# Seven block products for a graph product, spread over a batch of an attention loop

## The chip, the cores and the metric

The kernel runs on one core of a Trainium2 chip. A core has five engines with a queue each: TensorE (PE, matrix products; its weight loads are listed as PEld), VectorE (DVE), ScalarE (ACT), GpSimd (POOL) and SyncE (SP, which here only issues DMAs). Each engine works through its own queue in order, and semaphores make one queue wait for another. The metric is the time of one execution on the device, in microseconds, from the first to the last instruction and what lies around them; lower is better.

## The reference

Two layers work on 16 batches of 1024 rows by 256 channels, all in fp32. The change lies in the first layer and touches its seams to the second. Cut to what matters:

```python
def layer0(x, para, adj, kv_w):            # x: (16, 1024, 256)
    fea = transpose(x, (0, 2, 1))
    c = mean(fea, axis=1)                  # mean over channels, one per row
    diff = c[:, None, :] - c[:, :, None]
    A = abs(abs(sigmoid(diff) - 0.5) - 0.5) * 2.0
    A_s = (A + transpose(A, (0, 2, 1))) * 0.5
    g = einsum('bcn,bnm->bcm', fea, adj[None] * A_s)   # the graph product
    g = relu(g * para.reshape(1, 256, 1024))
    q = g transposed, 4 heads of 64
    k, v = x @ kv_w, 4 heads of 64
    attn = softmax(q k^T * scale)
    return attn @ v

x = layernorm(x + layer0(x, ...))
x = layernorm(x + layer1(x, ...))          # adjacency average, two linear layers, batchnorms
```

## The kernel before

A batch is 1024 rows in eight chunks of 128 partitions (`NCH`), so a batch's x is a tile of 128 x 8 x 256. Everything of the first layer runs in one loop over *bursts*. A *unit* is one head pair (64-channel heads, two at a time), one half of the queries and one chunk of 128 keys; a batch has 32 units, a burst is two of them, and so a batch has 16 bursts, called 0 to 15 here (`u` in the code). Bursts 0 to 7 are head pair 0, bursts 8 to 15 head pair 1.

In each burst PE first computes the scores of the burst's two units (`scores`, L903), for which ACT takes the exponential (L908); then the outputs of the burst before (`outputs`, L924), beside which DVE sums the exponentials into `acc` (L931, L933), one accumulation of 1024 wide a unit and none for the first unit of a query half. When a query half is through (once in four bursts), ACT copies half of its output (L937) and DVE adds the other half (L938). When a head pair is through, `normalise` multiplies `acc` with ones on PE (L946) to get the denominators, ACT copies them out (L952), and SP sends them through DRAM to be turned into columns. Some bursts later `residual` transposes the outputs back on PE (L970), DVE scales them (L974), and POOL adds them to x (L979). After the second head pair's residual, `finish_x1` does the layernorm on DVE (L596, L597, L600, with a power on POOL, L589) and POOL stores the result.

Beside this attention of batch b, the loop prepares batch b+1. That preparation is a list of steps made by `prologue`:

- `begin` (L747 to L756): DVE sums x over channels, SP sends the means through DRAM and spreads them as a row `crow` over all partitions.
- `transpose_x` (L765, L768): PE transposes x into `xT`, DVE copies it out of PSUM.
- `keys` (L842, copied by ACT L846) and `values` (L855, copied by DVE L859).
- the weights of the graph product, in place in eight tiles `wg` of 128 x 1024: `weights_abs` on ACT (L784), `weights_tanh` on ACT (L789), `weights_adj` on DVE (L793, times the adjacency).
- `graph_mm` (L805): four results (two channel halves by two query halves), each of eight matmuls over the chunks, 32 in all; then `queries`: DVE multiplies by para and the scale (L814), ACT takes the relu (L817). Batch 0 has `graph_first` instead, which runs before the loop.

Which step is run in which burst is written out by hand. The sets `FULL` and `SIDE` say it: in bursts 0, 4, 6, 8, 10 and 12 four steps each of keys, values and graph matmuls, with transposes of the next batch but one in bursts 10 and 12; in bursts 13, 14, 15, 1, 2, 3 and beside the steps of 0 and 4 the abs, tanh and adjacency products. The queues of PE, ACT and DVE keep that written order within a stage; POOL and SP wait for data and buffers alone.

Buffers set the rest of the order. PSUM has two tiles of 1024 for scores (`tile_s`), two banks for everything else that is copied out (`tile_t`: transposes, keys, values, graph results, denominators, residuals), which alternate, and two for outputs. There are four tiles for exponentials (`pp`), one buffer `xT`, one `crow`, eight `wg`, three of x.

After the loop, the second layer builds its averaged features, from batch 1 on with a scheme of seven block products in place of eight (`left_sums` on POOL, L659 to L662; `right_sums` on DVE, L666 to L669; `products`).

Of the kernel before, what the change touches and what calls it, by code (L numbers as in the profile page):

```python
# [515 lines left out]
def fast_path(  # L516
# [74 lines left out]
    def layernorm(t, name):  # L591
        st = small.tile([P, NCH, 6], F32, tag="ln_st", name=f"st_{name}")
        mv = small.tile([P, NCH, 2], F32, tag="ln_mv", name=f"mv_{name}")
        rstd = small.tile([P, NCH], F32, tag="ln_rs", name=f"rs_{name}")
        for n in range(NCH):
            nc.vector.bn_stats(st[:, n, :], t[:, n, :])  # L596
            nc.vector.bn_aggr(mv[:, n, :], st[:, n, :])  # L597
        rsqrt(rstd, mv[:, :, 1], EPS)
        for n in range(NCH):
            nc.vector.tensor_scalar(  # L600
                t[:, n, :], t[:, n, :], mv[:, n, 0:1], rstd[:, n : n + 1], ALU.subtract, ALU.mult
            )

# [96 lines left out]
    with (  # L700
        tc.tile_pool(name="l0c", bufs=1) as l0c,
        tc.tile_pool(name="qkv", bufs=2) as qkv,
# [30 lines left out]
        def prologue(b):  # L733


            s = st[b]
            xt = s["x"]
            first, steps, side = [], [], []

            def step(f, *a):  # L740
                steps.append((f, a))
# [16 lines left out]
            def transpose_x(c, half):  # L758
                if c == 0 and half == 0 and b:
                    begin()  # L760
                if c == 0 and half == 0:
                    s["xT"] = xTp.tile([P, CC, N], F32, tag="xT", name=f"xT_{b}")
                pt = tile_t(f"pxT_{b}_{c}_{half}")
                for j in range(4):
                    nc.tensor.transpose(  # L765
                        pt[:, j * P : (j + 1) * P], xt[:, 4 * half + j, c * P : (c + 1) * P], ident
                    )
                nc.vector.tensor_copy(s["xT"][:, c, half * HALF : (half + 1) * HALF], pt)  # L768
# [28 lines left out]
            def graph_mm(c, half, part):  # L797
                if part == 0:
                    s["pg"] = tile_t(f"pg_{b}_{c}_{half}")
                    if c == 0 and half == 0:  # L800
                        s["qT"] = qkv.tile([P, CC, N], F32, tag="qT", name=f"qT_{b}")
                ps = s["pg"]
                hs = slice(half * HALF, (half + 1) * HALF)
                for n in (2 * part, 2 * part + 1):
                    nc.tensor.matmul(  # L805
                        ps, xt[:, n, c * P : (c + 1) * P], s["wg", n][:, hs],
                        start=(n == 0), stop=(n == NCH - 1),
                    )
                if part == 3:
                    queries(c, hs, ps)  # L810

            def queries(c, hs, ps):
                q = s["qT"][:, c, hs]
                nc.vector.scalar_tensor_tensor(  # L814
                    q, ps, -scale, para_s[:, c, hs], op0=ALU.mult, op1=ALU.mult
                )
                nc.scalar.activation(q, q, AF.Relu)  # L817

            def graph_first(n):

                if n == 0:
                    both = tile_s("pg_0_0")
                    s["pg"] = [both[:, H0], both[:, H1], tile_o("pg_0_1_0"), tile_o("pg_0_1_1")]
                    s["qT"] = qkv.tile([P, CC, N], F32, tag="qT", name="qT_0")
# [6 lines left out]
                if n == NCH - 1:  # L831
                    for c in range(CC):
                        for half, hs in enumerate((H0, H1)):
                            queries(c, hs, s["pg"][2 * c + half])

            def keys(kc, half):
                if kc == 0 and half == 0:
                    s["kT"] = qkv.tile([P, CC, N], F32, tag="kT", name=f"kT_{b}")
# [7 lines left out]
                nc.scalar.copy(s["kT"][:, kc, hs], ps)  # L846

            def values(pair):
                if pair == 0:
                    s["v"] = qkv.tile([P, NCH, C], F32, tag="v", name=f"v_{b}")  # L850
                pt = tile_t(f"pv_{b}_{pair}")
                for j in range(2):
# [6 lines left out]
                nc.vector.tensor_copy(  # L859
                    s["v"][:, 2 * pair : 2 * pair + 2, :].rearrange("p n c -> p (n c)"), pt  # L860
                )

            for i in range(2 * CC):
                first.append((transpose_x, (i // 2, i % 2) if b else (i % 2, i // 2)))
            if b == 0:
                first += [(begin, ()), (row_of_means, ())]
            for i in range(4):
                step(values, i)
                step(keys, i // 2, i % 2)
            for c in range(CC):  # L870
                for half in range(2):
                    for part in range(4):
                        if b:
                            step(graph_mm, c, half, part)
            for n in range(NCH if b == 0 else 0):
                step(graph_first, n)
            for n in range(NCH):
                side.append((weights_abs, (n,)))
                side.append((weights_tanh, (n,)))
                if n:  # L880
                    side.append((weights_adj, (n - 1,)))
            side.append((weights_adj, (NCH - 1,)))
            return first, steps, side
# [11 lines left out]
        def scores(i):  # L895
            b, pr, qh, m = units[i]
            qT, kT = st[b]["qT"], st[b]["kT"]
            ps = tile_s(f"ps_{i}")
            for kh in range(2):
                for hd in range(2):  # L900
# [3 lines left out]
                        ps[kh * D : (kh + 1) * D, hd * HALF : (hd + 1) * HALF], kT[r, pr, ks],  # L904
                        qT[r, pr, qh * HALF : (qh + 1) * HALF], start=True, stop=True,
# [34 lines left out]
        def normalise(b, pr):  # L940
# [10 lines left out]
            row = rdp.tile([P, HALF], F32, tag="drow", name=f"drow_{k}")  # L951
# [28 lines left out]

        def finish_x1(b):
            xt = st.pop(b)["x"]
            layernorm(xt, f"l0_{b}")
            nc.gpsimd.dma_start(x1_d[b], xt)
# [129 lines left out]
        FULL = (0, 4, 6, 8, 10, 12)  # L1114
        SIDE = {13: 2, 14: 2, 15: 2, 1: 2, 2: 2, 3: 2}
        with tc.manual_schedule(engines={mybir.EngineType.PE, mybir.EngineType.Activation, mybir.EngineType.DVE}):


            first, steps, side = prologue(0)
            run(first, 6)  # L1120
            next_first, next_steps, next_side = prologue(1)
            for _ in range(8):
                run(steps, 1)
                run(side, 2)
            run(next_first, 4)
            for n in range(NCH):
                run(side, 2)
                run(steps, 1)
                if n:
                    run(next_side, 3)  # L1130
            run(next_side, 99)
            run(next_steps, 8)
            full, sums, late = {}, {}, {}

            def back(j):
# [4 lines left out]
                if m == NCH - 1 and qh == 1:  # L1140
                    sums.setdefault(j + 1, []).append((normalise, (b, pr)))
                    for q in range(2):
                        full.setdefault(j + 5, []).append((residual, (b, pr, q)))
                    if pr == PAIRS - 1:
                        late.setdefault(j + 6, []).append((finish_x1, (b,)))
# [5 lines left out]
                8: [(transpose_adjacency, (m, h)) for m in (6, 7) for h in (0, 1)],  # L1151
                5: [(load_x1l, (0,))],
# [7 lines left out]
                6: [(adjacency_rows, (n,)) for n in (0, 1, 2)] + [(load_weights, ())],  # L1160
# [4 lines left out]
            for j in range(len(bursts)):  # L1165
# [3 lines left out]
                if u == 0:  # L1169
                    steps, side = next_steps, next_side  # L1170
                    next_first, next_steps, next_side = [], [], []
# [3 lines left out]
                if u == 5 and b + 2 < B:  # L1175
                    load_x(b + 2)
                    next_first, next_steps, next_side = prologue(b + 2)
                if u in FULL:
                    if u >= 10:
# [406 lines left out]
```

## Time and profile before

| what | value |
|---|---|
| median of three runs | 2655.48 us (2652.28 to 2655.86) |
| the profiled execution | 2653.06 us |
| its span, first to last instruction | 2651.3 us |
| before the attention loop | 75.4 us |
| attention loop, batches 1 to 13 | 104.9 us each |
| from the last burst to the end | about 1020 us |

A line of a profile names the source line, the engine, the operation and its tiles by the program's names, output first. A fp32 matmul of the source shows as two passes in the profile, so 32 matmuls of a batch are 64. Groups give a mean duration of one; where instructions of an engine follow each other without a wait, the next can start before the first has ended. The idle time of an engine that isn't on the path that sets the end costs nothing.

In the page's slices of the span, an engine's busy share is a digit (tenths) for each of 40 stretches of 66 us; the attention loop fills stretches 2 to 26:

```profile
DVE  5465665756656657666566576765655655533376
ACT  5363563654645636545446354410101001233368
POOL 0001000100100011001000100321222211100044
```

In the loop DVE is busy for some six tenths, ACT for five, POOL for less than one.

### The profile page before, as it was taken

How to read it: one execution, taken by the hardware profiler on the slowest of the kernel's cores; microseconds unless marked ns; L12 is line 12 of the kernel's file. 1: busy time of each engine (PE TensorE's matmuls, PEld its weight loads, DVE VectorE, ACT ScalarE, POOL GpSimd, SP SyncE). 2: the span in 40 equal slices, each digit the busy share in tenths (PEclk: the TensorE clock that was granted, in tenths of full speed). 3: DMA queues.
4: the chain of work that ended last, by engine and by line, in shares of the span. 5: the costliest groups of instructions: out<-in, count | busy, mean ns of one | idle time of the engine just before them, and what ended most of it. 6: DMA issues, size and time to landing. Idle time of an engine off the chain costs nothing. (4 is left out here: it accounts for less than half of the span.)

```text
span 2651.3 us, 31994 instructions
## 1 busy us (share of the span) xinstructions
PE 2553.7 (96%) x12966; PEld 1110.1 (42%) x12966; DVE 1600.2 (60%) x2160; ACT 1126.8 (43%) x1349; POOL 336.2 (13%) x407
## 2 busy tenths in 40 slices
PE   8999999999999999999999999999999999999964
PEld 4443444444434434444444343344444444444443
DVE  5465665756656657666566576765655655533376
ACT  5363563654645636545446354410101001233368
POOL 0001000100100011001000100321222211100044
PEclk9999999999999999999999999999999999999975
DMA  4001101001011011010110110112122122353367
GB/s 143 2 9 41 33 10 41 21 22 33 9 41 33 9 41 33 10 41 3 39 33 9 41 49 1 41 64 95 80 95 95 66 92 82 137 202 143 149 222 240
DMA packets 134557, 168.94 MB, mean 64 GB/s; under 512 B 86785, under 2 KB 120065, under 8 KB 124033
## 3 DMA queue, kind: packets, MB, share of 16 engines
q1 hardware_dynamic: 129568, 116.47, 14.2%
q0 software_dynamic: 4832, 50.34, 4.6%
q8 instruction: 103, 1.69, 0.3%
q14 instruction: 54, 0.43, 0.0%
HBM read 99.36 MB, written 67.44 MB: 63 GB/s over the span
## 5 line engine op out<-in xcount | busy, mean ns | idle before, releaser
L908 ACT ACTIVATE p<-ps 128x1024 f32<-128x1024 f32 x512 | 495.7, 1020 | 179.5 <-PE ps L903 142.9
L933 DVE TENSOR_TENSOR acc<-acc,p 128x1024 f32<-128x1024 f32 x384 | 483.2, 1258 | 61.0 <-ACT p L908 32.4
L903 PE MATMUL ps<-qT,kT 64*64 64x512 f32 x4096 | 490.6, 594 | 1.4 <-ACT p L908 1.4
L924 PE MATMUL po<-p,v 64*64 64x512 f32 x4096 | 485.3, 589 | 0.0
L805 PE MATMUL pg<-wg,x 128*128 128x512 f32 x960 | 425.2, 596 | 0.0
L979 POOL TENSOR_TENSOR x<-x,o 128x512 f32<-128x512 f32 x64 | 109.5, 1711 | 1434.8 <-DVE o L974 1434.8
L924 PEld LDWEIGHTS po<-p,v 64*64 64x64 f32 x4096 | 156.7, 133 | 282.8 <-issue 282.6
L805 PEld LDWEIGHTS pg<-wg,x 128*128 128x128 f32 x960 | 177.6, 190 | 226.9 <-issue 203.3
L903 PEld LDWEIGHTS ps<-qT,kT 64*64 64x64 f32 x4096 | 146.1, 132 | 280.2 <-issue 231.5
L817 ACT ACTIVATE qT<-qT 128x512 f32<-128x512 f32 x64 | 40.3, 631 | 482.0 <-DVE qT L814 481.9
L1456 PE MATMUL po<-hl,w12T 128*128 128x512 f32 x512 | 220.3, 592 | 3.1 <-ACT hl L1387 2.3
L814 DVE SCALAR_TENSOR_TENSOR qT<-pg,para_s 128x512 f32<-128x512 f32 x64 | 43.9, 689 | 271.1 <-PE pg L805 269.8
L793 DVE SCALAR_TENSOR_TENSOR wg<-wg,adj_s 128x1024 f32<-128x1024 f32 x128 | 153.1, 1217 | 15.5 <-ACT wg L789 15.5
L784 ACT ACTIVATE wg<-crow,ccol 128x1024 f32<-128x1024 f32 x128 | 146.6, 1146 | 11.8 <-DMA crow<-c 11.8
L1456 PEld LDWEIGHTS po<-hl,w12T 128*128 128x128 f32 x512 | 97.1, 190 | 126.3 <-issue 120.5
L789 ACT ACTIVATE wg<-wg 128x1024 f32<-128x1024 f32 x128 | 135.5, 1060 | 2.6
L1387 ACT ACTIVATE hl<-hl,bn_sh,bn_sg 128x1024 f32<-128x1024 f32 x64 | 74.3, 1229 | 135.0 <-DMA hl<-h 133.6
L855 PE MATMUL pv<-kvw_s,xT 128*128 128x256 f32 x512 | 124.0, 385 | 1.6 <-ACT kT L846 1.6
L1460 DVE TENSOR_SCALAR o<-po,col_b 128x1024 f32<-128x1024 f32 x32 | 41.1, 1284 | 139.1 <-PE po L1456 139.1
L842 PE MATMUL pk<-xT,kvw_s 128*128 128x512 f32 x256 | 120.3, 592 | 0.0
L855 PEld LDWEIGHTS pv<-kvw_s,xT 128*128 128x128 f32 x512 | 94.9, 190 | 51.9 <-issue 27.6
L1286 PE MATMUL a_agg<-ahT,x1l 128*128 128x512 f32 x240 | 108.1, 593 | 1.1 <-ACT agg L1104 1.1
(151 smaller groups left out, 2625.4 us busy)
## 6 DMA issues: line engine op xcount, KB each, us to landing
h<-hw POOLq DMA_DIRECT2D x16, 2048.0 KB, 6.6
hl<-h SPq DMA_DIRECT2D x15, 2048.0 KB
x<-x POOLq DMA_DIRECT2D x16, 1024.0 KB, 4.2
x1l<-x SPq DMA_DIRECT2D x16, 1024.0 KB
xf<-x SPq DMA_DIRECT2D x16, 1024.0 KB
out_dram<-o SPq DMA_DIRECT2D x16, 1024.0 KB
x<-in_x_dram SPq DMA_DIRECT2D x15, 1024.0 KB
crow<-c SPq DMA_DIRECT2D x15, 512.0 KB
```

Source lines behind the costliest of these rows:

```text
L784: nc.scalar.activation(w, s["crow"], AF.Abs, bias=s["ccol"][:, n : n + 1])
L789: nc.scalar.activation(w, w, AF.Tanh, scale=0.5)
L793: nc.vector.scalar_tensor_tensor(w, w, 1.0, adj_s[:, n, :], op0=ALU.subtract, op1=ALU.mult)
L805: nc.tensor.matmul(ps, xt[:, n, c * P : (c + 1) * P], s["wg", n][:, hs], start=(n == 0), stop=(n == NCH - 1),)
L842: nc.tensor.matmul(ps, kvw_s[:, c, kc * P : (kc + 1) * P], s["xT"][:, c, hs], start=(c == 0), stop=(c == CC - 1),)
L855: nc.tensor.matmul(pt[:, j * C : (j + 1) * C], s["xT"][:, c, n * P : (n + 1) * P], kvw_s[:, c, C : 2 * C], start=(c == 0), stop=(c == CC - 1),
L903: nc.tensor.matmul(ps[kh * D : (kh + 1) * D, hd * HALF : (hd + 1) * HALF], kT[r, pr, ks], qT[r, pr, qh * HALF : (qh + 1) * HALF], start=Tr ...
L908: nc.scalar.activation(p, ps, AF.Exp)
L924: nc.tensor.matmul(g["po"][kh][hd * D : (hd + 1) * D, :], s["v"][r, m, h * D : (h + 1) * D], p[r, hd * HALF : (hd + 1) * HALF], start=(m = ...
L933: nc.vector.tensor_add(g["acc"], g["acc"], p)
L979: nc.gpsimd.tensor_tensor(xs, xs, o.rearrange("p n h d -> p n (h d)"), ALU.add)
L1456: nc.tensor.matmul(ps[:, hs], w2T[:, k, c * P : (c + 1) * P], h[k][:, hs], start=(k == 0), stop=(k == HC - 1),)
```

## The change

The change rewrites the preparation of a batch and its places in the loop.

The graph product of batches 1 to 15 is made of seven block products of four matmuls each (`graph`, `product`), 28 matmuls in place of 32. For it DVE forms four sums of the weights (`right_first` to `right_fourth`, 16 subtractions of 512 wide a batch), and POOL four sums of x (`left`, 512 wide), which lie in the buffer of `xT`. The seven results are added up in the query tiles by one ACT copy and seven DVE additions; the product with para moves to POOL (`times_para`, four a batch), and the scale goes into ACT's relu.

The weights of batch b+2 are begun in bursts 11 to 15 of batch b (abs and tanh), their products with the adjacency follow about one burst behind the tanh, the sums behind these, into burst 6 of the next batch. The graph products sit in bursts 4 (one), 6, 8 and 10 (two each), the transposes of x in burst 10, keys and values in bursts 12 and 14, just ahead of the batch's attention. One half of the copies of `xT` and of the values goes from DVE to ACT.

The layernorm is split: statistics (DVE, POOL) five bursts after the last burst of a batch, the last step two bursts later and on ACT, as eight Identity activations with scale and bias. The residual of the second head pair comes one burst earlier. Query and key tiles are held by head pair, three buffers each; the row of denominators shares a buffer with the scaled outputs; loading the second layer's weights moves from batch 14 to batch 15; two small tiles of statistics move into other pools. Before the loop, batch 1's transposes, keys and values are no longer made; batch 0's order is changed a little.

```diff
     def layernorm(t, name):
...
+        def statistics():
+            for n in range(NCH):
+                nc.vector.bn_stats(st[:, n, :], t[:, n, :])
+                nc.vector.bn_aggr(mv[:, n, :], st[:, n, :])
+            rsqrt(rstd, mv[:, :, 1], EPS)
+            nc.gpsimd.tensor_tensor(nmr, mv[:, :, 0], rstd, ALU.mult)
+            nc.gpsimd.tensor_scalar(nmr, nmr, -1.0, None, ALU.mult)
+
+        def apply(n):
+            nc.scalar.activation(
+                t[:, n, :], t[:, n, :], AF.Identity,
+                bias=nmr[:, n : n + 1], scale=rstd[:, n : n + 1],
             )
...
-                nc.vector.tensor_copy(s["xT"][:, c, half * HALF : (half + 1) * HALF], pt)
+                copy = nc.scalar.copy if half and b else nc.vector.tensor_copy
+                copy(s["xT"][:, c, half * HALF : (half + 1) * HALF], pt)
...
+            def right_first(i):
...
+                nc.vector.tensor_sub(S["t1"][:, i, :], w[:, H1], w[:, H0])
+
+            def right_second(i):
+                nc.vector.tensor_sub(S["t2"][:, i, :], s["wg", i + LOW][:, H1], S["t1"][:, i, :])
...
+            def left(k):
+                if k == 0:
+                    S["l"] = xTp.tile([P, 4, LOW, P], F32, tag="xT", name=f"xS_{b}")
...
+                nc.gpsimd.tensor_tensor(l[k], one, two, op)
+
+            def product(k):
+                ps = tile_t(f"pg_{b}_{k}")
+                w = [s["wg", i] for i in range(NCH)]
+                for i in range(LOW):
+                    one, two = {
+                        1: lambda: (xt[:, i, C0], w[i][:, H0]),
...
+                        7: lambda: (S["l"][:, 2, i, :], w[i][:, H1]),
+                    }[k]()
+                    nc.tensor.matmul(ps, one, two, start=(i == 0), stop=(i == LOW - 1))
+                return ps
...
+            def times_para(c, half):
...
+                nc.gpsimd.tensor_tensor(q, q, para_s[:, c, hs], ALU.mult)
...
+                if k == 5:
+                    nc.vector.tensor_add(u, ps, u)
+                    nc.vector.tensor_add(v, ps, v)
+                    times_para(1, 1)
+                if k == 3:
+                    nc.vector.tensor_add(u, ps, u)
+                    times_para(0, 1)
...
+                copy = nc.scalar.copy if pair % 2 and b else nc.vector.tensor_copy
+                copy(s["v"][:, 2 * pair : 2 * pair + 2, :].rearrange("p n c -> p (n c)"), pt)
...
+                "kv": [
+                    (values, (0,)), (keys, (0, 0)), (values, (1,)), (keys, (0, 1)),
+                    (values, (2,)), (values, (3,)), (keys, (1, 0)), (keys, (1, 1)),
+                ],
...
+                "graph": [(graph, (k,)) for k in (1, 6, 2, 7, 4, 5, 3)],
...
+            for i in range(LOW):
+                two = (i, i + LOW)
+                for n in two:
+                    side += [(weights_abs, (n,)), (weights_tanh, (n,))]
+                todo["adj"] += [(weights_adj, (n,)) for n in two]
+                todo["sums"] += [(f, (i,)) for f in (right_first, right_second)]
+            todo["sums"] += [(f, (i,)) for f in (right_third, right_fourth) for i in range(LOW)]
...
+                    wait = 5 if j == len(bursts) - 1 or pr == 0 else 4
                     for q in range(2):
-                        full.setdefault(j + 5, []).append((residual, (b, pr, q)))
+                        full.setdefault(j + wait, []).append((residual, (b, pr, q)))
                     if pr == PAIRS - 1:
-                        late.setdefault(j + 6, []).append((finish_x1, (b,)))
+                        late.setdefault(j + 5, []).append((statistics_x1, (b,)))
+                        late.setdefault(j + 7, []).append((finish_x1, (b,)))
...
+                if u < 4:
+                    part("left", 1)
+                part("side", 99 if u == 0 else 0)
+                part("adj", {0: 1, 1: 99}.get(u, 0))
+                part("sums", {0: 1, 1: 3, 2: 2, 3: 1, 4: 1, 5: 2, 7: 99}.get(u, 0))
+                if u == 4:
+                    part("graph", 1)
+                elif u == 6:
+                    part("graph", 2)
+                    part("sums", 2)
+                elif u == 7:
+                    part("relu", 1)
+                elif u == 8:
+                    part("graph", 2)
+                elif u == 9:
+                    run(after.get("begin", []), 1)
+                elif u == 10:
+                    part("graph", 2)
+                    part("xT", 4)
+                elif u == 11:
+                    part("relu", 3)
+                    run(after["side"], 4)
+                elif u == 12:
+                    for i in range(4):
+                        part("kv", 1)
+                        run(after["side"], 1 + i % 2)
+                        run(after["adj"], i % 2)
+                elif u == 13:
+                    run(after["side"], 2)
+                    run(after["adj"], 2)
+                elif u == 14:
+                    for i in range(4):
+                        part("kv", 1)
+                        run(after["side"], 1)
+                        run(after["adj"] if i % 2 else after["sums"], 1)
+                elif u == 15:
+                    run(after["adj"], 1)
+                    run(after["sums"], 2)
+                run(full.get(j, []), 9)
```

## The prediction

> **What bounds the kernel now.** I read the page's head first, then stages by windows, then the attention loop burst by burst, then the timeline where engines hand over.
>
> ```profile
> PE 2553.7 (96%) x12966; PEld 1110.1 (42%) x12966; DVE 1600.2 (60%) x2160; ACT 1126.8 (43%) x1349; POOL 336.2 (13%) x407
> ...
> 267.30:372.20 104.90, 104.31 (x679) 43.57 (x675) 66.49 (x88) 54.76 (x63) 9.45 (x7) 1.00 0.10 26
> ```
>
> The second line is one batch of the attention loop (length, then busy time of PE, weight loads, DVE, ACT, POOL): PE works 104.3 of 104.9 us, so every wait added to PE is lost time. Batches 1 to 13 all take 104.9; batch 0 takes 87.0, batch 14 104.5, batch 15 74.1 to its last burst's scores. The loop starts at 75.4. Cut at its 16 bursts, one batch reads (bursts 4, 5, 6, 8, 12):
>
> ```profile
> 708.87:720.83 11.96, 11.72 (x69) 6.47 (x61) 7.12 (x10) 6.38 (x8) 0.00 (x0) 1.00 0.00 0
> 720.83:724.31 3.48, 3.48 (x33) 1.28 (x36) 2.21 (x4) 1.94 (x2) 2.64 (x2) 1.00 0.00 0
> 724.31:734.92 10.61, 10.61 (x52) 4.03 (x45) 8.12 (x26) 1.94 (x2) 3.35 (x4) 1.00 0.06 22
> ...
> 738.40:750.01 11.61, 11.61 (x61) 4.19 (x53) 3.98 (x5) 2.87 (x5) 0.00 (x0) 1.00 0.27 90
> ...
> 768.41:781.45 13.04, 12.69 (x69) 5.75 (x61) 5.56 (x8) 3.15 (x4) 0.00 (x0) 1.00 0.14 42
> ```
>
> A burst with scores and outputs alone takes 3.43 to 3.48. Burst 6 adds 8 graph matmuls, two passes each, 0.429 start to start in the timeline: 6.86. 3.43 + 6.86 = 10.29, so a burst with other PE work also pays 0.32 for the change of tile form, and 0.05 in the next. Burst 8 adds the denominators (0.86 + 0.13). Burst 12 adds 16 transposes of 0.109 (1.74), which leaves 0.69 of waiting; burst 4 adds 8 (0.87), which leaves 0.48.
>
> The groups of the page give the prices (busy time, mean ns of one; then idle time before it and what ended it):
>
> ```profile
> L908 ACT ACTIVATE p<-ps 128x1024 f32<-128x1024 f32 x512 | 495.7, 1020 | 179.5 <-PE ps L903 142.9
> L784 ACT ACTIVATE wg<-crow,ccol 128x1024 f32<-128x1024 f32 x128 | 146.6, 1146 | 11.8 <-DMA crow<-c 11.8
> L789 ACT ACTIVATE wg<-wg 128x1024 f32<-128x1024 f32 x128 | 135.5, 1060 | 2.6
> ```
>
> The view of tile aT has a DVE subtraction alone (ns least/median/most); the timeline, in the second layer, has the same shape beside POOL's left sums, and in the attention loop accumulations beside one POOL residual:
>
> ```profile
> L666 DVE TENSOR_TENSOR aT<-ahT x4: 677/682/684, 1735.0 to 1742.5; 128x512 f32<-128x512 f32 x4
> ```
>
> ```profile
> 1782.35 1.14 DVE L666 TENSOR_TENSOR tT<-agg 128x512 f32<-128x512 f32 x1
> 1782.91 1.70 POOL L661 TENSOR_TENSOR x1S<-x1l 128x512 f32<-128x512 f32 x1
> ...
> 1783.52 1.64 DVE L667 TENSOR_TENSOR tT<-agg,tT 128x512 f32<-128x512 f32 x1
> 1784.57 1.71 POOL L660 TENSOR_TENSOR x1S<-x1S,x1l 128x512 f32<-128x512 f32 x1
> 1785.08 1.75 DVE L668 TENSOR_TENSOR tT<-agg 128x512 f32<-128x512 f32 x1
> 1786.36 1.59 POOL L662 TENSOR_TENSOR x1S<-x1l,x1S 128x512 f32<-128x512 f32 x1
> ...
> 680.12 6.11 DVE L933 TENSOR_TENSOR acc<-acc,p 128x1024 f32<-128x1024 f32 x4
> ```
>
> The reader sees: the same DVE subtraction takes 0.68 alone and 1.64 to 1.75 while POOL runs a two-input operation; the two engines take turns. In the attention loop, too: four accumulations take 6.11 when one POOL residual falls among them, 5.20 elsewhere, so 0.9 for each POOL operation. Back to back, ACT starts follow each other by 0.92 (exp), 1.18 (abs, its tanh next), 0.96 (tanh), 1.04 (abs, something else next), 0.48 (copy), 0.54 to 0.60 (relu), 0.49 (256-wide Identity); DVE by 1.14 (1024 wide) and 0.60 (512).
>
> [...]
>
> **Part by part, per batch.**
>
> Removed from PE: 4 of 32 graph matmuls, 8 passes x 0.429 = 3.43. Also gone are the two waits behind residuals: in burst 12 the pool of two banks waited for a query (0.69), in burst 4 for a key copy (0.48). Added: bursts with other PE work go from six (0, 4, 6, 8, 10, 12) to eight (0, 3, 4, 6, 8, 10, 12, 14): 2 x 0.37 = 0.7. So without new waits 104.9 - 3.43 - 1.17 + 0.7 = 101.0.
>
> Added to DVE: 16 subtractions (9.6) and 7 additions for 4 query products (1.8 more); removed: the layernorm step (2.7), half of the x and v copies (2.4). About 66.5 + 6.3 = 73. ACT: 54.8 + 8 Identity (3.9) + 5 copies (2.4) = 61. POOL: 8 two-input operations of 1.26 to 1.75 more. All below 101 over a batch; what counts is when.
>
> New wait 1, burst 10. Four transposes follow the last product in the two banks. The product's end E, DVE add to E+0.9, then transpose group 2; group 3 waits for DVE's copy (E+1.55), group 4 for ACT's (E+2.25), end E+2.69 against 1.74: 0.95.
>
> New wait 2, burst 12. ACT now has three relus, then abs, tanh, abs, tanh in burst 11, all ahead of burst 12's exps and copies. With burst 12's start as 0: burst 11's exps start at -2.38, the next operation at -0.54, relus to 1.2, two pairs of 2.15 to 5.5, exps to 7.34, the oT copy ends 7.93. DVE in order: oT add to 8.6, values(0) copy to 9.3. PE could start values(1) at 7.1 and gets its bank at 9.35: 2.25 lost. keys(0,1) and the first residual find banks free; the second residual waits 0.4 for ACT's last key copy. Sum about 2.6; burst 13 starts at 14.15. Bursts 13 to 15 then fit: exp of 13 is 0.35 late, under its slack. Unknown: 1.5 if the relus and copies slip earlier, 3.2 if a relu waits for POOL's product with para.
>
> New wait 3, burst 0. The four left sums on POOL need only that the keys and values have left the shared buffer, so all four start behind burst 14's last key matmul, whatever burst they are written in: at 0.1 after burst 15's start, four in a row. DVE is then in two-input work. It leaves values(2)'s copy at -4.4, then two sums and two adjacency products (3.46) to -0.94, then accumulation, accumulation, adjacency, two sums, two accumulations: 6.0 without POOL. Four turns of 0.93 make it 9.7. Before, four steps of PE work stood ahead of burst 0's denominators; now nothing does, and PE, ready at 3.48 + 3.43 = 6.9, waits 2.8. Bounds: below 0 is excluded, since DVE has 0.9 to spare without POOL; if two sums come later, 0.9; with 1.07 a turn, 3.4. Queued behind on PE: denominators, then burst 1's scores. Taken: 2.8.
>
> At no cost: the parameter products and residuals on POOL (DVE is in PSUM copies or ahead); ACT's eight Identities in burst 6 (3.9 beside 10.6 of PE); statistics in burst 4 (4.2 of DVE; exp of burst 6 is 0.4 late under 10.6); the x store and load in burst 6 (SP blocked until about 12 us after its start, next needed at burst 9). The row of means: issue to issue took 8.5 to 11.0, and 3.8 from issue to ACT's start at 39.13; begin in burst 9 gives the row 3 us before the first abs. If that cover goes, ACT stops in burst 11.
>
> Sum: 101.0 + 0.95 + 2.6 + 2.8 = 107.35, against 104.9: +2.45 in each of batches 1 to 13: +31.9. Batch 14 has no weights to come (wait 2 all but gone): +0.3. Batch 15: +0.5 (one more tile change). Batch 0 takes over keys, values and transposes of batch 1 and graph tile changes: 107.35 less burst 0 and the missing residual, 98.7 from burst 1 on, against 84.8: +13.9. The start loses the same work: batch 1's row lands at about 42.5 as now, 14 abs and tanh follow at 1.07, then relus, two more, two copies: burst 1 at about 62.4 instead of 77.6: -15.2. At the end ACT's eight Identities stand behind DVE statistics and POOL's power before copies that PE needs: 0 to 8, taken 3. Together -1.3 + 31.9 + 0.3 + 0.5 + 3 = +34. The profiled execution took 2653.06 (span 2651.3), 0.1% under the median shown, so 2687 there and 2688 beside the median.
>
> **Rivals.**
>
> POOL does not hold DVE: the left sums run spread over bursts 0 to 3 or lose their turns, wait 3 goes: 34 - 14 x 2.8 = -5: 2651. For it: they are written one a burst; against: only buffers hold POOL.
>
> ACT's queue is absorbed (wait 2 gone, POOL's hold stays): 34 - 14 x 2.6 = -2: 2653. For it: ACT is busy only 61 of 107; against: the queue is in order.
>
> PE stays the bound, the other side: every burst ends on PE because ACT reaches burst 12's oT copy before PE reaches values(1) and DVE ends its accumulation before the denominators. Place: bursts 12 and 0; price: -41, so 2614. It decides from an ACT queue under about 5.2 us behind burst 12's start and a DVE end under 6.9. For it: no burst loses more than 0.7 today; against: both sums above pass these points by over 2 us.
>
> **How the numbers follow.** Forecast 0.45, POOL free 0.18, ACT absorbed 0.12, PE bound 0.25. The likeliest's own range is 2662 to 2704 (waits 2 and 3 at their ends, the tail, 5 us at the start). To leave out no more than 2 in 10 the range must reach the PE-bound case: 2613 to 2704. A measurement tells 0.2% (5.3 us) from no change. Faster: 0.25 + 0.08 + 0.03 + 0.02 = 0.38; same 0.07 + 0.05 + 0.03 = 0.15; slower 0.40 + 0.03 + 0.04 = 0.47.
>
> **What would show it.** In the changed profile: graph passes 840 instead of 960; values(1) idle behind a DVE copy of v in burst 12, about 2 us; denominators idle behind DVE acc in burst 0, about 2.8, with four POOL left sums of 1.7 side by side with slow DVE operations; a batch of 107.4. The forecast is wrong if a batch takes 102 and PE is busy throughout.

## The result and the profile after

The changed kernel takes 2724.55 us (median of four runs, 2722.12 to 2726.85), the kernel before 2655.16 (2652.28 to 2655.86) on the same chip: a ratio of 1.0263, 95% interval 1.0246 to 1.0281. It is slower, by 69 us. The forecast was 2688, and its range ended at 2704. The profiled execution's span went from 2651.3 to 2725.1: +73.8.

The page of the changed kernel, first the engines' busy time, then the slices of the span:

```profile
PE 2559.7 (94%) x12846; PEld 1089.6 (40%) x12846; DVE 1789.0 (66%) x2257; ACT 1233.8 (45%) x1552; POOL 577.5 (21%) x559
...
DVE  5686776867867768668677686575655555533376
ACT  6466465554664655546646464521101110233368
POOL 1021221322212213222121231242111111100034
```

PE has 120 passes fewer and yet is busy for 6.0 us more (2553.7 before): passes that do the same work must have become longer somewhere. DVE is up from six tenths of the loop to seven, POOL from less than one to nearly two.

The windows of the same kernel: one batch (6, counted from 0) whole, then its bursts 0, 4, 6, 8, 10 and 12. Columns: stretch, length, busy time with instruction counts of PE, weight loads, DVE, ACT, POOL, then granted TensorE clock, DMA share and GB/s.

```profile
712.46:820.51 108.05, 102.97 (x668) 41.94 (x664) 79.43 (x95) 61.64 (x75) 25.45 (x18) 1.00 0.10 26
712.46:720.62 8.16, 5.58 (x45) 1.36 (x37) 8.02 (x7) 2.52 (x3) 4.03 (x3) 1.00 0.00 0
732.10:739.33 7.23, 7.23 (x42) 2.57 (x41) 5.81 (x9) 2.53 (x3) 3.45 (x2) 1.00 0.00 1
742.81:753.42 10.61, 10.61 (x53) 4.03 (x45) 6.12 (x8) 5.98 (x10) 5.75 (x5) 1.00 0.00 0
756.90:768.50 11.60, 11.60 (x60) 4.18 (x52) 6.39 (x7) 2.77 (x4) 0.11 (x1) 1.00 0.30 92
771.99:785.37 13.38, 12.96 (x69) 5.79 (x61) 6.74 (x11) 2.52 (x3) 2.53 (x2) 1.00 0.17 6
788.85:802.92 14.07, 11.99 (x69) 6.39 (x61) 6.05 (x9) 13.83 (x18) 0.02 (x1) 1.00 0.00 0
```

The batch that had 104.9 us with PE busy for 104.3 now has 108.05 with 103.0: work went out, waits came in. Two bursts hold most of them: in burst 0 PE is idle for 2.6 us while DVE works 8.02 of 8.16, in burst 12 for 2.1 us while ACT works 13.83 of 14.07.

But of the batches 1 to 13 this is the only one with 108; ten take 109.4 to 109.7 and two 111.1. The windows of bursts 0 and 1 of batch 5, the batch before, show why:

```profile
603.02:612.05 9.03, 6.45 (x45) 1.41 (x37) 8.89 (x8) 2.53 (x3) 4.03 (x3) 0.87 0.00 0
612.05:616.05 4.00, 4.00 (x34) 1.40 (x36) 3.97 (x6) 2.52 (x3) 0.00 (x0) 0.86 0.11 3
```

The same 45 PE instructions are busy for 6.45 us in place of 5.58, and the granted clock of the stretch is 0.87. The trace's record of the clock has a stretch of 3.41 us at 0.5 here, from 609.7. Batches 1 to 13 have twelve such half-clock stretches, two of them double, 47.8 us together, and batch 14 one more; in the loop of the kernel before there were none. A batch with a single one takes 1.4 to 1.6 us more than one without.

Why batch 5 and not batch 6, with the same wait? The stretches start on a grid with steps of 3.41 us (from 282.0 to 609.7 they are 109.2 us apart, 32 steps), and what differs is how the wait lies on it. These are the grid's windows around the two waits; the clock fell at the end of the first and not at the end of the second:

```profile
606.30:609.72 3.42, 1.31 (x8) 0.14 (x4) 3.31 (x3) 0.59 (x1) 0.83 (x1) 1.00 0.00 0
715.53:718.94 3.41, 1.52 (x12) 0.14 (x4) 3.31 (x3) 0.59 (x1) 1.04 (x1) 1.00 0.00 0
```

PE was busy for 1.31 us of the first window and for 1.52 of the second.

The largest waits of PE in the loop by line (total, times, longest) and the timeline behind the first; in the timeline rows of other instructions are left out, "x2" is two instructions in a row, and the bracket is the idle time before with what ended it:

```profile
PE den L1048 <- DVE acc L1035: 36.2, 14, 2.7
PE pv L947 <- DVE v L952: 25.7, 14, 1.8
PE pah L1154 <- ACT ahT L1157: 8.6, 4, 7.6
```

```profile
708.00 3.54 DVE L1035 TENSOR_TENSOR acc<-acc,p 128x1024 f32<-128x1024 f32 x2
709.18 3.49 POOL L837 TENSOR_TENSOR xS<-x 128x512 f32<-128x512 f32 x2 [10.06 <-ACT wg L791]
711.46 2.29 DVE L800 SCALAR_TENSOR_TENSOR wg<-wg,adj_s 128x1024 f32<-128x1024 f32 x1
712.63 2.25 POOL L837 TENSOR_TENSOR xS<-xS,x 128x512 f32<-128x512 f32 x1
713.68 1.75 DVE L813 TENSOR_TENSOR t<-wg 128x512 f32<-128x512 f32 x1
714.96 1.60 POOL L837 TENSOR_TENSOR xS<-x,xS 128x512 f32<-128x512 f32 x1
715.47 1.65 DVE L816 TENSOR_TENSOR t<-wg,t 128x512 f32<-128x512 f32 x1
716.00 1.05 PE L1048 MATMUL den<-acc,ones 128*32 128x512 f32 x4
717.04 2.54 DVE L1035 TENSOR_TENSOR acc<-acc,p 128x1024 f32<-128x1024 f32 x2
719.63 1.05 PE L1048 MATMUL den<-acc,ones 128*32 128x512 f32 x4 [2.58 <-DVE acc L1035]
```

Burst 0 of batch 6 starts at 712.46. The left sums of POOL (`xS`) run in one row from just after burst 15's start (708.98), one DVE operation is slow beside each (2.29 for 1.22, 1.75 and 1.65 for 0.68), and the second half of the denominators comes when DVE's last accumulation is through.

Added up by where a stretch begins and ends, the 73.8 us are: the start to burst 1 of batch 0 -16.2, the rest of batch 0 +16.7, batches 1 to 13 +62.8, batch 14 +2.9, batch 15 +7.6, behind the loop 0. (From the end of the last burst's scores to the end it is 946.6 us in both kernels; the table of the kernel before says "about 1020", which is the time from the last batch's start.)

### The profile page after: what moved, and what is told of

Read it like the earlier page. It is cut to its first block, busy times and chain, and to the rows that moved or that the text cites. A ratio compares the mean times of both kernels' runs of the same rounds, so it can differ in the third digit from the quotient of the medians.

```text
span 2725.1 us, 32299 instructions
## 1 busy us (share of the span) xinstructions
PE 2559.7 (94%) x12846; PEld 1089.6 (40%) x12846; DVE 1789.0 (66%) x2257; ACT 1233.8 (45%) x1552; POOL 577.5 (21%) x559
## 3 DMA queue, kind: packets, MB, share of 16 engines
q1 hardware_dynamic: 129568, 116.47, 13.9%
## 5 line engine op out<-in xcount | busy, mean ns | idle before, releaser
L1010 ACT ACTIVATE p<-ps 128x1024 f32<-128x1024 f32 x512 | 497.9, 1020 | 285.7 <-PE ps L1005 229.7
L1035 DVE TENSOR_TENSOR acc<-acc,p 128x1024 f32<-128x1024 f32 x384 | 498.1, 1297 | 42.6 <-ACT p L1010 19.2
L1005 PE MATMUL ps<-q,k 64*64 64x512 f32 x4096 | 509.1, 614 | 5.3 <-ACT p L1010 3.7
L1005 PEld LDWEIGHTS ps<-q,k 64*64 64x64 f32 x4096 | 146.6, 137 | 306.0 <-issue 279.2
L800 DVE SCALAR_TENSOR_TENSOR wg<-wg,adj_s 128x1024 f32<-128x1024 f32 x128 | 184.4, 1459 | 21.2 <-ACT wg L796 21.2
L872 POOL TENSOR_TENSOR q<-q,para_s 128x512 f32<-128x512 f32 x60 | 81.7, 1362 | 425.1 <-DVE q L896 186.7
L852 PE MATMUL pg<-wg,x 128*128 128x512 f32 x360 | 163.4, 596 | 0.0
L1076 DVE TENSOR_TENSOR o<-poT,r_all 128x512 f32<-128x512 f32 x64 | 44.3, 692 | 103.1 <-PE poT L1072 61.9
L852 PE MATMUL pg<-t,xS 128*128 128x512 f32 x240 | 111.0, 605 | 0.0
L852 PE MATMUL pg<-wg,xS 128*128 128x512 f32 x240 | 109.5, 599 | 0.0
```

The lines of the kernel that those rows point to most:

```text
L800: nc.vector.scalar_tensor_tensor(w, w, 1.0, adj_s[:, n, :], op0=ALU.subtract, op1=ALU.mult)
L852: nc.tensor.matmul(ps, one, two, start=(i == 0), stop=(i == LOW - 1))
L1005: nc.tensor.matmul(ps[kh * D : (kh + 1) * D, hd * HALF : (hd + 1) * HALF], kT[r, ks], qT[r, qh * HALF : (qh + 1) * HALF], start=True, stop ...
L1010: nc.scalar.activation(p, ps, AF.Exp)
L1035: nc.vector.tensor_add(g["acc"], g["acc"], p)
```

## The experiments

The theory after the result had three parts: DVE's and POOL's work collides ahead of burst 0's denominators; ACT's queue delays burst 12; and the wait in burst 0 has a second price, TensorE's clock. All ratios are to the kernel before, with 95% intervals. None of these kernels leaves out a part of the computation.

**The left sums held back.** They are made to wait for burst 0's denominators, by two copies of one column on POOL whose result the sums overwrite.

```diff
+                    if "row" in G:
+                        for q in (0, 2):
+                            nc.gpsimd.tensor_scalar(
+                                S["l"][:, q, 0, 0:1], G["row"][:, 0:1], 1.0, None, ALU.mult
+                            )
...
+            G["row"] = row
...
-                if u < 4:
+                if 1 <= u < 5:
                     part("left", 1)
```

> The four left sums on POOL are made to wait for the denominators' row of burst 0 (two copies of one element of it, overwritten by the sums), so they run in bursts 1 to 3. Theory: POOL's hold on DVE in bursts 15 and 0 delays the last accumulations, PE waits some 3.5 us for them before the denominators, and that wait halves PE's clock for a window. Then burst 0 falls from 8.2 to 9.0 us to about 4.7, burst 1 from 3.5 to 5.6 us to 3.5, no granted clock of 0.5 remains between 200 and 1600 us, a batch takes 104.7 instead of 109.7 and the whole about 2656. Rival: DVE is late by its own added sums and adjacency products, POOL apart: burst 0 stays at 8 us or more and the whole above 2712.

Measured: 2690.16 us, ratio 1.0136 (1.0119 to 1.0153). Its windows of bursts 0 and 4:

```profile
698.80:703.34 4.54, 4.54 (x45) 1.23 (x37) 3.17 (x4) 2.53 (x3) 0.00 (x0) 1.00 0.00 0
715.05:724.16 9.11, 7.53 (x41) 2.47 (x41) 7.44 (x12) 3.55 (x4) 2.81 (x2) 1.00 0.00 1
```

Burst 0 fell from 8.16 to 4.54 with PE busy throughout, and none of the batches 1 to 14 had a half-clock stretch any more. So POOL's sums, where they stood, are needed for the wait. But most of the loss moved: burst 4 went from 7.23 to 9.11, burst 3 up by 0.24, burst 6 by 0.65, because the same turns now delay DVE's accumulations and with them exponentials (ahead of burst 4 ACT waits 3.78 us for one). 3.6 us were won in a batch and 2.8 given back; most of the 34 us that the whole gained is the clock. The expected 2656 did not come.

**One pair of abs and tanh moved from burst 11 to burst 13.**

```diff
                     part("relu", 3)
-                    run(after["side"], 4)
+                    run(after["side"], 2)
...
-                    run(after["side"], 2)
+                    run(after["side"], 4)
```

> One abs and tanh pair fewer in burst 11, one more in burst 13. Theory: ACT's queue of burst 11 makes burst 12's output copy late, behind it DVE's copy of the first values, for which PE waits: burst 12 falls from 14.07 to about 12.0 (2.15 us of ACT gone), burst 0 is as in the changed kernel, the whole about 2695. Rival: the two PSUM banks turn over too slowly for eight copies in any case: burst 12 stays at 13.5 or more, the whole above 2715.

Measured: 2686.74 us, 1.0126 (1.0109 to 1.0142). Burst 12 fell from 14.07 to 12.41, which is ACT's queue: 1.66 us a batch. Burst 0 was 8.17 as before, but now only five of the batches 1 to 14 had a half-clock stretch: 106.4 us without, 108.1 with. The same wait, in batches of another length, hits the clock less often; that made up the rest of the gain, some 14 of 38 us.

**Four of the right sums moved from bursts 14 and 15 to bursts 2 to 4; POOL's sums stay.**

```diff
-                part("sums", {0: 1, 1: 3, 2: 2, 3: 1, 4: 1, 5: 2, 7: 99}.get(u, 0))
+                part("sums", {0: 1, 1: 3, 2: 4, 3: 2, 4: 2, 5: 2, 7: 99}.get(u, 0))
...
-                        run(after["adj"] if i % 2 else after["sums"], 1)
+                        run(after["adj"], i % 2)
                 elif u == 15:
                     run(after["adj"], 1)
-                    run(after["sums"], 2)
```

> The four first right sums move from bursts 14 and 15 to bursts 2 to 4, the left sums stay on POOL where they are. Theory: DVE has 2.4 us less ahead of the last accumulations, PE waits about 1.2 us before the denominators instead of 3.55, too short to halve the clock: burst 0 about 5.8, burst 1 3.5, no 0.5 clock in the loop, the whole about 2668. Rival (the halved clock has nothing to do with this wait): one window of 0.5 a batch stays and the gain is 2.4 us a batch at most, the whole at 2690. If POOL took no turns, the wait would have been gone altogether and burst 0 at 4.7.

Measured: 2661.09 us, 1.0027 (1.0015 to 1.0038); burst 0 4.58, burst 1 3.48, a batch 105.08. Its timeline ahead of the denominators of batch 6:

```profile
684.15 2.30 DVE L800 SCALAR_TENSOR_TENSOR wg<-wg,adj_s 128x1024 f32<-128x1024 f32 x1
686.45 4.43 DVE L1035 TENSOR_TENSOR acc<-acc,p 128x1024 f32<-128x1024 f32 x2
687.54 2.25 POOL L837 TENSOR_TENSOR xS<-xS,x 128x512 f32<-128x512 f32 x1
689.88 2.14 POOL L837 TENSOR_TENSOR xS<-x,xS 128x512 f32<-128x512 f32 x1
...
690.89 1.10 PE L1048 MATMUL den<-acc,ones 128*32 128x512 f32 x8
```

The run's own expectation for burst 0, about 5.8, missed, and by its last sentence 4.58 would mean that POOL takes no turns. The timeline says otherwise: POOL still takes them, two accumulations in a row take 4.43 in place of 2.54, and yet all eight denominators passes find their sums ready, with nothing to spare (the last accumulation ends at 690.88). The expectation had counted the moved sums at 0.6 each, but two of them had stood beside POOL and taken 1.75 and 1.65. So the wait needs both, DVE's added work and POOL's turns; with either gone from this place, burst 0 is whole. That a wait of 1.2 us is too short to halve the clock was an estimate, and with no wait left it was not tried here; in the changed kernel the clock stayed full behind each of burst 12's 14 waits of 1.84 us. The move was worth 63 us of the 69 that the change had cost; burst 6 pays 0.6 a batch for it (11.22 for 10.61).

**The wait kept, the idle time filled.** Is it the idle time that costs the clock? The second of the four denominators matmuls is repeated inside the wait, writing the same numbers again. First with six repeats:

```diff
-            for i in range(4):
+            for i in ((0, 1) + (1,) * (6 * pr) + (2, 3)):
                 nc.tensor.matmul(
                     den[i * 32 : (i + 1) * 32, :], ones[:, :32],
```

> The second denominators matmul of head pair 1 is repeated six times (twelve passes of about 0.21 us, 2.6 us, same result) inside the wait of burst 0, so PE is never idle there for more than about 1 us; the wait for the accumulation itself stays. Theory (the idle time of 3.5 us halves TensorE's clock in 12 windows of the middle batches, 3.41 us of half work each): burst 0 stays at 8.17 us in every batch, burst 1 at 3.48, every batch 1 to 13 at 108.0, half-clock time in the loop falls from 68.3 to about 17 us, the time falls by about 24 to 2700 us. Rival (the clock windows have nothing to do with the idle time, or their cost comes from elsewhere): batches stay mostly at 109.7, the time at 2724. Second rival (the added passes delay the path): burst 0 above 8.5.

Measured: 2734.09 us, 1.0304 (1.0286 to 1.0321). Slower, and still it tells the two apart: every batch from 1 to 13 took 109.57 or 109.58, burst 1 was 3.48, and half-clock time in the loop fell from 68.3 to 17.1 us. But burst 0 was 9.68: the repeats ended 1.5 us too late, since one pass of the same block takes 0.43 us from start to start, not 0.21. With three repeats, and only where the wait is:

```diff
-            for i in range(4):
+            for i in ((0, 1) + (1,) * (3 if pr and b < B - 2 else 0) + (2, 3)):
```

> The kernel with six repeats of the second denominators matmul kept the clock full, but its twelve passes took 0.43 us each from start to start (not 0.21, the mean of a group whose rows overlap) and ended 1.5 us after the accumulation. Here it is three repeats (six passes, 2.57 us, inside the wait of about 3.5 us), and only for the denominators of batches 0 to 13, behind which the wait stands. Theory (the idle time itself halves the clock): burst 0 at 8.17 in each of batches 1 to 14, burst 1 at 3.48, batches 1 to 13 at 108.05 each, half-clock time in the loop about 17 us; the changed kernel's batches 1 to 14 lie 23.3 us above that, so the time is 2724.5 - 23.3 = 2701 us. Rival (the full clock needs the whole wait filled, or the repeats only trade one loss for another): some batches at 109.7 with half-clock windows, the time above 2712.

Measured: 2701.00 us, 1.0178 (1.0161 to 1.0195). Its windows of batch 6 and of that batch's bursts 0 and 1:

```profile
702.59:810.64 108.05, 105.54 (x674) 42.60 (x670) 79.43 (x95) 61.64 (x75) 25.45 (x18) 1.00 0.10 26
702.59:710.75 8.16, 8.16 (x51) 2.02 (x43) 8.02 (x7) 2.52 (x3) 4.03 (x3) 1.00 0.00 0
710.75:714.23 3.48, 3.48 (x34) 1.27 (x36) 3.48 (x5) 2.52 (x3) 0.00 (x0) 1.00 0.06 7
```

Burst 0 is as long as with the wait (8.16) but PE is busy for all of it, the clock is 1.00, and batches 1 to 13 all take 108.05 to 108.16. Three useless matmuls a batch made the kernel 23.5 us faster (2724.55 - 2701.00). This is the price of the clock by itself; the wait for the accumulation is untouched.

**The last batch but one's layernorm step one burst later.**

```diff
-                        late.setdefault(j + 7, []).append((finish_x1, (b,)))
+                        late.setdefault(j + (8 if b == B - 2 else 7), []).append((finish_x1, (b,)))
```

> Only the last batch but one's layernorm step goes one burst later (from burst 6 to burst 7 of batch 15). Theory (in batch 15 the eight Identities stand in ACT's queue ahead of the copies of the adjacency's transposes and wait for POOL): batch 15 falls from 81.7 to about 73.6 us, burst 6 from 14.1 to about 6.2, nothing else moves, the time is 2724.5 - 8 = 2716.5 us. Rival (the copies wait for something else and the wait moves on to bursts 7 and 8): batch 15 stays within 2 us of 81.7, the time above 2722.

Measured: 2717.65 us, 1.0247 (1.0229 to 1.0264); batch 15 fell from 81.71 to 73.51, its burst 6 from 14.13 to 6.14. Two more things moved: burst 7 fell from 5.18 to 3.49, since the half-clock stretch of 10.24 us behind the long wait is gone too, and burst 9 rose from 7.40 to 8.88. What it removes stands in the changed kernel's timeline of batch 15:

```profile
1727.66 2.68 POOL L589 TENSOR_TENSOR rs_l<-rs_l,mhalf 128x8 f32<-128x8 f32 x1
...
1730.42 1.11 POOL L603 TENSOR_TENSOR nm_l<-mv_l,rs_l 128x8 f32<-128x8 f32 x1
1731.62 1.28 POOL L604 TENSOR_SCALAR nm_l<-nm_l 128x8 f32<-128x8 f32 x1
1732.93 4.04 ACT L607 ACTIVATE x<-x,nm_l,rs_l 128x256 f32<-128x256 f32 x8 [3.40 <-POOL nm_l L604]
...
1737.60 1.97 PE L1154 MATMUL pah<-ident,adj_s 128*128 128x128 f32 x8 [7.60 <-ACT ahT L1157]
```

The eight Identities wait for POOL's small operations, stand in ACT's queue ahead of the copies of the adjacency's transposes, and PE waits 7.60 us for a bank.

**Combinations.** First, the held-back left sums with the moved pair and the later layernorm step:

> Both edits together, and in the last batch the layernorm's last step one burst later, behind the copies of the adjacency transposes. Theory: the waits add up independently: a batch of about 102.6, burst 6 of batch 15 about 8 instead of 14.1 and its burst 7 3.5, the whole about 2620, faster than before by 1.3%. Rival (the waits hide one another, or the left sums only move DVE's delay to bursts 2 to 4): a batch of 104 or more, the whole no faster than 2645.

Measured: 2661.53 us, 1.0028 (1.0019 to 1.0038). The expected 2620 did not come. Bursts 3, 4 and 6 keep what the held-back sums cost (4.80, 9.10, 11.26), and the clock's loss, gone already with the held-back sums, can't be won again by the moved pair.

Second, the later right sums with the moved pair and the later layernorm step:

> The sums of bursts 14 and 15 moved to 2 to 4 (as in the run with that edit alone), one abs and tanh pair from burst 11 to 13, and the last step of the layernorm one burst later in the last batch. Theory: the three waits are separate, so their gains add up: burst 0 at 4.6, burst 12 at 12.4, a batch at 103.4 instead of 105.08, batch 15 at 75 instead of 81.4, the whole about 2661 - 14 x 1.66 - 6.4 = 2631. Rival (ACT's pair in burst 13 makes a new wait once DVE is lighter): burst 14 longer than 10.7, the whole above 2645.

Measured: 2630.79 us, ratio 0.9907 (0.9891 to 0.9924): faster than both kernels, and by some 24 us faster than the one before. Its page's busy line:

```profile
PE 2523.6 (96%) x12846; PEld 1103.4 (42%) x12846; DVE 1774.9 (68%) x2257; ACT 1230.8 (47%) x1552; POOL 557.7 (21%) x559
```

PE is busy for 30 us less than before the change, and its share is 96% again. A batch takes 103.44.

**Three attempts at the rest of burst 12.** The first half of each output's copy moves from ACT to DVE: on top of the fastest version, then with two right sums also moved from burst 4 to burst 7, then alone in the changed kernel.

```diff
-                nc.scalar.copy(g["oT"], g["po"][0])
+                nc.vector.tensor_copy(g["oT"], g["po"][0])
```

> As the run before, and the output's first half is copied by DVE instead of ACT. Theory: with that DVE's copy of the first values stands behind no ACT work, and ACT reaches the key copies in time: burst 12 falls to about 11.6, a batch to 102.6, the whole to about 2620. Rival (the banks' turnover): burst 12 stays at 12.2 or more.

> As the run before, with the two sums of burst 4 left to burst 7. Theory: burst 6's 0.6 us above 10.61 is PE waiting for the bank that a late DVE holds, behind statistics and sums of bursts 2 to 5: burst 6 at 10.61, a batch 0.6 less, the whole about 8 us less than the run before. If the statistics alone are it, burst 6 stays at 11.2.

> The changed kernel with nothing but the output's first half copied by DVE. Two readings of burst 12: if only the chain output copy on ACT, output addition and first value copy on DVE makes PE wait, burst 12 falls from 14.07 to about 11.9. If ACT's whole queue is late, the key and value copies on ACT hold the two banks as before and the last residual waits for the last key copy: burst 12 about 13.4. Burst 0 stays at 8.2 to 9.0.

Measured: 2647.14 (0.9969, 0.9957 to 0.9982), 2647.10 (0.9972, 0.9961 to 0.9984) and 2717.36 (a single execution). In the first two burst 12 stayed at 12.42, burst 6 took 11.40, bursts 5 and 6 lost 0.8 together: both were misses. What is left of burst 12's wait in the fastest version isn't the output's copy but the last of the key copies on ACT, as its timeline shows:

```profile
659.81 0.66 PE L1072 MATMUL poT<-ident,oT 128*128 128x128 f32 x4 [0.70 <-ACT k L938]
```

Alone in the changed kernel the move took burst 12 from 14.07 to 13.29, near the 13.4 expected if the whole queue of ACT stands ahead: one copy less is 0.8 less. There bursts 5 and 6 stayed at 3.48 and 10.61, so what they lost in the first two comes of the move together with the later right sums; this, and what the move costs behind the loop (949.4 in place of 946.9), was not followed further.

## Why the prediction went wrong

The direction and the likeliest case were right; under half of the time was foreseen, 34.4 of the span's 73.8 us. The step that failed is new wait 3, burst 0, the sentence "PE, ready at 3.48 + 3.43 = 6.9, waits 2.8". Its mechanism is shown: four left sums in one row behind burst 14's last key matmul, in turns with DVE, and the denominators behind the last accumulation; with POOL's half or DVE's half removed, it is gone. Its price was wrong in two ways.

- *The wait.* In the prediction's terms it is the time from PE's readiness to the last accumulation's end, 9.7 - 6.9. Counted from burst 15's start (708.98), PE was ready at 7.0, but DVE ended at 10.6: burst 0 went from 4.58 to 8.16, 3.58 longer and not 2.8. Two things made DVE late, by the timeline: the four turns cost 0.97 to 1.19 us each from start to start, not 0.93 (the second-layer lines of the prediction gave up to 1.07), and accumulations in a row follow each other by 1.32 (2.54 for two, 1.22 for one), not 1.14. That PE's idle time, 2.58, comes near the 2.8 is luck: PE did the first half of the denominators (1.05) inside the longer wait. It won nearly nothing by it. The four matmuls write four blocks of 32 columns; all eight passes take 1.10 us where nothing waits (the version with later right sums), and the second half still takes 1.05. In the traces the passes of such a row start 6 to 7 ns apart, four at a time in the kernel before (from 749.01) and two at a time in the changed kernel's wait (from 719.63), and the next ones 0.43 to 0.45 us later either way. Against the 107.35 us forecast for a batch the batch without a clock stretch is 0.7 longer: 9 us over 13 batches.
- *The clock, which no term of the sum had.* The wait lets the granted TensorE clock fall to 0.5 for 3.41 us, in most batches. The experiment that only fills the idle time recovers 23.5 us, of which 22 lie in batches 1 to 13: this is the largest part of the miss of 39 us. The prediction took a wait at the price of its length. The trace shows the grid: stretches of 3.41 us at 0.5, starts 109.2 us apart (32 windows) from 282.0 to 609.7 although the batches between are 109.65 to 109.69 long. Of the 3.41 us at 0.5 a batch lost 1.64 (109.69 - 108.05), about half. A gap of 2.58 us was enough for a fall, and the window before a fall wasn't wholly idle, as the last section shows.

The other terms, by the sum:

- *New wait 1, burst 10*: 13.38 measured; 10.61 for two products, 1.74 for the transposes and 0.95 of wait make 13.30.
- *New wait 2, burst 12*: 14.07 for the forecast 14.15. The chain was the one named, relus and two pairs ahead of exponentials and the output's copy. PE waited 1.84 for the values' bank and 0.24 for the last key copy, where 2.25 and 0.4 were counted; its own work took 0.5 longer than counted, so the close match is in part luck. The one-pair move gave 1.66 back.
- *Batch of 101.0 without new waits*: right where it can be seen. Burst 3 took 4.56 (3.43 + 0.87 + 0.37 = 4.67 by the prices used), burst 4 7.23 (3.43 + 3.43 + 0.32 = 7.18), burst 6 10.61 (3.43 + 6.86 + 0.32).
- *Batch 0 and the start*: -15.2 forecast and -16.2 measured; +13.9 and +16.7. Nearly all of the second difference is the clock as well: a half-clock stretch from 60.17 to 67.00 covers 5.55 us of burst 1, which took 6.22. In the other eleven kernels with this start burst 1 took 4.82 to 6.46, and in all twelve it is 3.45 to 3.53 plus half of what such a stretch covers.
- *Batch 14*: +0.3 forecast, +2.9 measured: the longer wait, and a clock stretch (1.4, as the filled kernel's 105.95 against 107.35 shows).
- *Batch 15*: "+0.5 (one more tile change)" was 7.6. The work listed at no cost had "ACT's eight Identities in burst 6 (3.9 beside 10.6 of PE)". In batch 15 that cover isn't there: what is in burst 6 are transposes whose copies stand behind the Identities on ACT. The sum was made for each engine's busy time there, not along ACT's queue. Here too the wait brought a half-clock stretch. One burst later it is all gone (73.51).
- *The end*: +3 forecast, 0 measured.

Of the rivals, "PE stays the bound" was wrong by its own test, as PE loses more than 2 us in each of bursts 0 and 12. "POOL does not hold DVE" and "ACT's queue is absorbed" were both refuted in the changed kernel, though kernels with one of the two waits removed exist now: 2661 (by DVE's half) and 2687. The forecast for the first, 2651, came within 10 us of what the removal gave; that for the second, 2653, was 34 too low, as wait 3 stays there with its clock.

## What to carry to other kernels

A wait of TensorE can have two prices, its length and the clock: 2.6 us of idle time inside a dense loop cost about another 1.6 us in thirteen of fourteen batches, and filling it with useless matmuls won that back without touching the wait. When work is moved onto two engines that take turns (DVE's subtraction took 1.65 to 1.75 us beside POOL's sums, 0.68 alone), look for the shared moment where someone waits for the later of the two; moving a few operations of one of them by four bursts was worth 63 us here, while holding back the other moved most of the wait's loss to later bursts. And what is "hidden beside other work" must be asked for each queue and for the first and the last batch apart, where the cover is different.

## What the runs showed of the hardware

- The clock's falls went with how busy PE was in a window of the grid, not with one gap's length. In batches 1 to 15 of the changed kernel the clock fell 14 times, each time behind a window of 3.41 us in which PE was busy for 0.71 to 1.51 us; of the other windows at the full clock, behind which it stayed, the least busy had 1.52, and in the loop of the kernel before, where it never fell, 2.08. So the border lay at about 1.5 us, 44% of a window: an estimate from these two traces, in which the ends of matmuls are modelled; no kernel was made to try it.
- This border accounts for both waits. A window that holds the whole wait of 1.84 us in burst 12 still has 1.57 of work (3.41 - 1.84); 1.62 is the least that was measured around these waits in the changed kernel, and the clock stayed full behind all of them. With the 2.58 of burst 0 it can go down to 0.83, and 0.83 was measured ahead of falls.
- The loss depends on the phase. With the same wait (burst 0 at 8.17) the changed kernel lost clock in thirteen of the batches 1 to 14, the version with the moved pair in five. A batch with a hit, 109.69 us, is 32.1 windows of 3.41, so the next batch meets nearly the same phase; a batch of 106.41 is 31.2 and slips. There one batch in three is hit: from 383.6 the falls come 320.9 us apart, which is 94 windows and three batches.
- A group's mean is not a pass's price where passes run side by side (in the kernel before the denominators' starts lie 6 to 7 ns apart, each pass recorded for 0.59 to 0.62 us): the same denominators pass counted 0.26 us in a row of four (1.05 / 4), 0.14 in a row of eight (1.10 / 8), and took 0.43 when repeated in one block.
- POOL's operations on 128 x 8 took 1.1 to 2.7 us each beside DVE accumulations, as long as one on 128 x 512 (1.3 to 2.3): four of them in a row, 6.4 us, were what ACT waited for in batch 15.
